# A fixed VectorE order in the last stage, earlier weight blocks spread out, and a root by Newton steps

## The chip, the cores and the metric

The kernel runs on one core of one Trainium2 chip. The metric is the time of one execution on the device in microseconds (us); the value given for a kernel is the median of its runs. In the text PE is TensorE (matrix products), DVE is VectorE, ACT is ScalarE (activation functions and copies), POOL is GpSimd, SP is the engine that issues most data transfers (DMAs). A tile here is 128 partitions of up to 512 float32 values for each of two halves of the 256 channels. "L712" is line 712 of the kernel before.

## The reference

The input is x of shape (2, 256, 64, 64) in float32. Two layers follow one another, each added to its own input, each after a group norm with 32 groups (8 channels to a group):

```python
x = x + layer0(group_norm(x))   # attention over 4096 positions, 8 heads of 32 channels
x = x + layer1(group_norm(x))   # grid attention, block attention, and a 3x3 convolution
```

Layer 0 is full attention: q, k, v by 1x1 convolutions, softmax over all 4096 positions, sums over v. Layer 1 computes q, k, v again, then

```python
ctx   = attention over positions (h % 8, w % 8) of each grid      # 64 groups of 64 tokens
feats = relu(bn(lr_W @ ctx))
qx = relu(bn(fq2 @ relu(bn(fq1 @ feats)))); kx = the same with fk1, fk2; vx = fv @ feats
out_att  = relu(bn(sr_W @ attention(qx, kx, vx)))                 # within 8x8 blocks
out_conv = conv3x3(fc(q, k, v heads), dep_w)
result   = rate1 * out_att + rate2 * out_conv
```

A group norm is `(x - mean) / sqrt(var + 1e-5)`, with mean and variance over 8 channels and all positions. Its root is computed per channel on 128 partitions, for the first 128 channels and for the second 128 channels apart.

## The kernel before, in words

The two batches are worked through one after the other, b = 0 and b = 1, and each has three stages.

Stage 1, attention of layer 0 (lines 400 to 920). PE makes the scores into a ring of PSUM banks (L594), ACT takes their exponentials (L600), PE sums them over v (L609), and DVE adds up the exponentials for the row sums (L646). Sixteen groups (8 heads, two halves of the queries) of 32 steps; `last` is the last group, and `at_block(last, j, f)` puts the work f behind step j of it. The order on PE, ACT and DVE is the order of the program (`manual_schedule`); on other engines a scheduler decides. While the last groups run, DVE gathers the statistics of the first 128 channels of layer 1's group norm: their mean and variance (`mean_of_first`, `variance_of_first`) are there by step 12. When the last scores have been taken, `before_last_rows` computes the root of the variance, its reciprocal and the shift `-mean * rstd`, and starts the normalisation of these channels (`Groups.normalise`, three tiles on POOL, five on ACT by `by_act`), while PE makes the last row sums. `behind_last_rows` takes the reciprocal of the row sums on DVE, copies them on ACT, and gives ACT the rest of the normalisations. The second 128 channels need the last head, so their mean, variance and root (`Stats.deviations`, L368) come after it. In batch 0 PE then multiplies weight matrices into each other (`fold_products`, L270 to L299: transposes, a copy on ACT called turned_w, products called pm_w) and DVE prepares the convolution's weights (prep, L984).

ACT holds one table of functions. Sqrt and Exp are in different ones, so a switch puts a table load on ACT, which the profile shows as ACT_TABLE_LOAD. The small tile `warm` is used to cause such a load ahead of time (L397 with Exp).

Stage 2, grid attention (`layer1_first`), follows for the 8 tiles: projections py (L1389), scores, softmax, feats.

Stage 3, `layer1_second`, runs over 8 tiles t of 512 positions (8 blocks of 64). Each makes hidden rows phq and phk, rows prq and prk, the values vs, scores sp, the softmax (nm, e, den, e on DVE with the exponential on ACT), its transpose at, the block matrix bd (DVE), and the result pc into res. Between these pieces PE runs convolution steps: `conv()` calls at up to three spots of a tile. The convolution is of Winograd form. Batch 0 uses F(2,3) along the rows and columns: 16 steps (strip s, column q). Batch 1 uses a wider form along the columns: 12 steps, c0 to c11, in the order (0,0)...(0,5),(1,5)...(1,0). One `conv()` issues the transform of the next step and the products of this one:

- col: POOL makes a difference of image columns, DVE finishes it with three operations (batch 1, L1155 to L1160), and there is one col buffer
- v: POOL makes four row terms of col (L1165)
- mm: 32 products on PE (L1180 for batch 1, L1062 for batch 0), into one PSUM tile of four banks, which must have been read before the next step writes it
- z: a copy on ACT and four operations on DVE (L1201 to L1204, batch 0 L1070 to L1073)
- additions of z into the layer's rows x, called xphase in batch 1 (L1211)

`conv_edges` then adds border terms to tile t on ACT, and `to_image` normalises a tile into the image xp. The block `with tc.manual_schedule(engines=...)` in this loop says on which engines the program order holds: PE always, DVE too where `near` holds (the last two tiles of batch 0). Elsewhere the scheduler interleaves DVE's instructions.

Batch 1's wider form needs two more sets of weights, which batch 0's stage 3 makes and stores: `wider_weights(wf, r, stage)` for r = 0 to 3, four DVE operations (L1102 to L1105) into the two halves of one staging tile and two transfers to memory (L1107, wf_more). A call must wait until the transfers of the call before have read the staging tile. Calls r = 0 and 1 come behind tile 3, r = 2 and 3 behind tile 4.

Of the kernel before, what the change touches and what calls it, by code (L numbers as in the profile page):

```python
# [35 lines left out]


ROWSUM_LO, ROWSUM_HI = 1e-18, 1e18


@with_exitstack
def direct_layers(ctx: ExitStack, tc: tile.TileContext, a: dict, out: bass.AP, bad: bass.AP):
# [102 lines left out]
    eps = const.tile([P, 1], F32, name="eps")  # L145
    nc.gpsimd.memset(eps, 1e-5)
    warm = const.tile([P, 1], F32, name="warm")

    def load_const(name, shape, src, behind=None):
        t = const.tile(shape, F32, name=name)  # L150
# [370 lines left out]
    def attention0(b, xts, held):  # L521
# [187 lines left out]

        def before_last_rows():  # L710

            nc.scalar.activation(st.rstd[:, first_chunk], st.d[:, first_chunk], AF.Sqrt, bias=eps)  # L712
            for t in range(2):
                st.tile(1, t)
            nc.vector.reciprocal(st.rstd[:, first_chunk], st.rstd[:, first_chunk])
            st.shift = small.tile([P, KC], F32, tag="gn_shift", name=f"shift_{b}")
            shift_of(st, 0)
            held["groups"] = Groups(es, xts, st)
            for t in range(NT - N_POOL, NT):
                held["groups"].normalise(0, t, nc.gpsimd)  # L720
            held["by_act"] = iter(range(NT - N_POOL))
            by_act(2)

        def by_act(n):
            for t in itertools.islice(held["by_act"], n):
                held["groups"].normalise(0, t, nc.scalar)

        def behind_last_rows(g):

            avs = copied[g] = w4([P, 2, T], f"avs_{b}_{g}")  # L730
            kept = held["kept"] = w4([P, T], f"kept_{b}")
            held["y"] = avs[:, 0, :]
            for part, at in enumerate(held["rows"]):
                n = slice(part * T // 2, (part + 1) * T // 2)
                for made in (nc.vector.reciprocal(avs[:, 1, n], ring[:, at, n]), nc.scalar.copy(kept[:, n], ring[:, at, n])):
                    for other in rows_made[1 - part]:
                        tc.declare_no_dep(made.ins, other.ins, reason="another bank of the ring")
                by_act(1 + part)
            for t in range(2, NT // 2):
                st.tile(1, t)  # L740

# [73 lines left out]
        at_block(last, 6, lambda: wanted.append(mean_of_first))  # L815
        at_block(last, 11, lambda: st.spread(first_chunk))
        at_block(last, 12, lambda: wanted.append(variance_of_first))

        for t in range(NT):
            if t >= NT // 2:  # L820
# [667 lines left out]
    def layer1_second(b, xts, feats, mean, rstd, shift, pacc, following):  # L1488
# [83 lines left out]
        for t in range(NT):  # L1572
            nt = f"sr_{b}_{t}"
            f = [
                feats[k][:, 8 * t : 8 * t + 8].rearrange("p o d e -> p (o d e)") for k in range(KC)
            ]

            def hidden(one, col1, nm):
                hid = w4([P, KC, T], f"h{nm}_{nt}")
                ph = [bank([P, T], f"ph{nm}_{nt}_{m}") for m in range(KC)]  # L1580
                for k, m in ((0, 0), (0, 1), (1, 0), (1, 1)) if t == 0 else ((0, 0), (1, 0), (0, 1), (1, 1)):
                    nc.tensor.matmul(  # L1582
                        ph[m], wts[one][:, k, m * P : (m + 1) * P], f[k], start=k == 0, stop=k == KC - 1
                    )
                    if k == KC - 1:
                        kept["rows"] = bn_relu(hid[:, m, :], ph[m], col1, m)
                return hid

            def branch(one, two, col1, col2, nm, between=None):
                hid = hids.pop(nm, None) or hidden(one, col1, nm)  # L1590
                if between:
                    between()
                res = w4([P, KC, T], f"r{nm}_{nt}")
                pr = [bank([P, T], f"pr{nm}_{nt}_{m}") for m in range(KC)]
                for k in range(KC):
                    for m in range(KC):
                        nc.tensor.matmul(  # L1597
                            pr[m], wts[two][:, k, m * P : (m + 1) * P], hid[:, k, :], start=k == 0, stop=k == KC - 1
                        )
                for m in range(KC):  # L1600
                    bn_relu(res[:, m, :], pr[m], col2, m)
                return res

            E = mybir.EngineType
            seam = b == 0 and t == NT - 1
            near = b == 0 and t >= NT - 2

            def step(n=1):
                for _ in range(n if near else 0):
                    next(then)  # L1610

            with tc.manual_schedule(engines={E.PE, E.DVE} if near else {E.PE}):
                hids = {}
                if t == 0:
                    hids = {"q": hidden("fq1", V_FQ1, "q"), "k": hidden("fk1", V_FK1, "k")}
                q = branch("fq1", "fq2", V_FQ1, V_FQ2, "q")
                if pending:
                    next(pending)
                    next(pending, None)
                    pending = None  # L1620
                with tc.issue_after(kept["rows"].ins):
                    for tt in images.get(t, ()):
                        to_image(tt)
                if 0 in spots.get(t, ()) and (b or t > 2):
                    conv(step if seam else None)
                if seam:
                    for n in sorted(results):
                        give(n)
                k = branch("fk1", "fk2", V_FK1, V_FK2, "k", step if seam else None)
                in_x = b and t % 4 == 0  # L1630
                res = xpool.tile([P, KC, T], F32, tag="x", name=f"res_{nt}") if in_x else w4([P, KC, T], f"res_{nt}")

                def to_res(m, pc, res=res):

                    bn_relu(
                        res[:, m, :].rearrange("p (d o e) -> p o d e", d=8, o=8),
                        pc.rearrange("p (o d e) -> p o d e", o=8, d=8), V_SRW, m,
                    )

                parts = group_attention(  # L1640
                    nt, q, k, lambda c, w, f=f: f[c][:, w * P : (w + 1) * P], wts["fv"], to_res, apart=t + 1 < NT,
                    split=t + 1 == NT, fill=lambda m: step(3 if seam else 0),
                )
                if seam:
                    step(5)
                if b == 0 and t == 2:
                    conv(behind_drain=lambda: next(parts))
                else:
                    next(parts)
                step()  # L1650
                if 1 in spots.get(t, ()):
                    conv(None if t < 2 and b == 0 else lambda: next(parts))
                elif b or t > 1:
                    next(parts)
                if t < 2 and b == 0:
                    pending = parts
                else:
                    if seam:
                        step(2)
                    next(parts, None)  # L1660
                    if seam:
                        for _ in then:
                            pass
                if 2 in spots.get(t, ()):
                    conv(step)
            if b == 0 and t == 1:


                with tc.issue_after(kept["seam"]):
                    kept["bias"] = conv_weights()  # L1670
                with tc.issue_after(kept["made"].ins):
                    for k in range(KC):
                        nc.vector.memset(xp[:, k, 0, :], 0.0)
                ahead[0] = conv_transform(b, xp, *turns[0])
            for tt in ((), (0, 1))[t] if b == 0 and t < 2 else (t,):
                conv_edges(xts, tt)
            if b == B - 1 and t == 2:
                report()
            results[t] = res
            if b:  # L1680
                for m in range(KC):
                    nc.vector.tensor_scalar(res[:, m, :], res[:, m, :], wts["rate1"], None, ALU.mult)
            if b == 0 and t in (3, 4):
                if t == 3:
                    stage = xpool.tile([P, KC, T], F32, tag="x", name="stage")
                with tc.issue_after(kept["bd"].ins):
                    for r in range(2 * (t - 3), 2 * (t - 3) + 2):
                        wider_weights(wf, r, stage)
            for n in sorted(n for n in results if done >= (NQ * (n // 4 + 1) if b else 4 * (n // 2 + 1))):
                give(n)  # L1690
            if b == 0 and t == NT - 3:
                next(then)
# [625 lines left out]
```

## Time and profile before

| | |
|---|---|
| median of 3 runs | 3011.64 us (3008.14 to 3016.84) |
| profiled execution | 3011.38 us, span 3009.5 us |
| PE | busy 2945.0 us (98%), 25043 matmuls |
| DVE | busy 2499.7 us (83%) |
| ACT | busy 2336.1 us (78%) |
| POOL | busy 815.0 us (27%) |
| PE's mean granted clock | 0.995 |
| DMA | 431.82 MB, mean 143 GB/s |

How to read it: the span is the time from the first to the last instruction that the profile sees, and the execution's own time has 1.9 us around it. A timeline line gives start and length in us, the engine, the line, the operation, the tiles written and read, how many instructions it stands for, and in brackets the idle time of the engine before it with what ended it. PEld is the load of weights into PE, which overlaps its products. The granted clock is the share of PE's full clock that it was allowed.

Stage 1 of batch 0 runs from about 113 to 1126 us, that of batch 1 to about 2637 us. Batch 0's convolution products lie between about 1300 and 1540 us, batch 1's between 2758 us and the end.

### The profile page before, as it was taken

To read this page: it belongs to the slowest core of one execution; us is meant where nothing else is said; L and a number is where in the kernel's file an instruction comes from. 1 tells how busy PE (TensorE), PEld (TensorE's weight loads), DVE (VectorE), ACT (ScalarE), POOL (GpSimd) and SP (SyncE) were. 2 spreads that over 40 slices of the span, in tenths; PEclk is the share of its full clock that TensorE was granted. 3 is DMA by queue.
4 is the path that set the end of the run, shared out by engine and by line. 5 is a ranking of instruction groups with operands and counts; after the bars stand their busy time and mean duration, and the time that the engine had idled before them with its cause. 6 is when DMAs were issued, how large, how long until landed. Compare 5 with 4: busy or idle time off the path is not lost.

```text
span 3009.5 us, 63901 instructions
## 1 busy us (share of the span) xinstructions
PE 2945.0 (98%) x25043; PEld 1830.7 (61%) x25043; DVE 2499.7 (83%) x3196; ACT 2336.1 (78%) x3283; POOL 815.0 (27%) x910
## 2 busy tenths in 40 slices
PE   7999999999999999998999999999999999998998
PEld 4555556665565656676765565566655656566665
DVE  4698998999899999956655989989998989955874
ACT  2699999999999994532235999999999999943433
POOL 1022222322222221065400232223222222213430
PEclk9999999999999999999999999999999999999999
DMA  7979778897888761231249797788978877720010
GB/s 257 277 139 184 148 157 168 160 190 149 164 181 161 154 145 43 62 139 64 63 171 264 147 182 146 163 166 162 187 147 170 176 156 151 154 69 22 15 57 30
DMA packets 254660, 431.82 MB, mean 143 GB/s; under 512 B 99416, under 2 KB 118668, under 8 KB 252172
## 3 DMA queue, kind: packets, MB, share of 16 engines
q0 software_dynamic: 96960, 237.57, 41.2%
q1 hardware_dynamic: 157244, 189.81, 23.1%
q8 instruction: 198, 3.24, 0.4%
q14 instruction: 114, 0.93, 0.1%
q10 hardware_dynamic: 144, 0.26, 0.0%
HBM read 124.27 MB, written 70.48 MB: 65 GB/s over the span
## 4 chain that ended last, share of the span: by engine, by line
PE 86%; DVE 6%; DMA 4%; ACT 2%; POOL 1%; issue 1%; SPq 0%; ACTq 0%; POOLq 0%; DVEq 0%
PE ring L594 32%; PE av L609 30%; PE mm L1062 3%; PE mm L1180 3%; PE p_wk L457 2%; PE p_wq L457 2%; DVE prep L984 2%; PE pv L483 2%; PE prq_sr L1597 1%; PE prk_sr L1597 1%; PE phk_sr L1582 1%; PE phq_sr L1582 1%; PE pvs_sr L1252 1%; DMA acc<-v 1%; PE ring L609 1%; PE pvs_lr L1252 1%
## 5 line engine op out<-in xcount | busy, mean ns | idle before, releaser
L600 ACT ACTIVATE es<-ring 128x512 f32<-128x512 f32 (+2 forms) x1574 | 1201.5, 906 | 35.8 <-PE ring L594 21.3
L594 PE MATMUL ring<-q,k 128*128 128x512 f32 x4096 | 1082.8, 407 | 7.9 <-ACT es L600 5.1
L646 DVE TENSOR_TENSOR e<-e,es 128x1024 f32<-128x1024 f32 (+1 forms) x942 | 1029.0, 1153 | 28.5 <-ACT es L600 27.0
L594 PEld LDWEIGHTS ring<-q,k 128*128 128x128 f32 x4096 | 731.3, 188 | 382.6 <-ACT es L600 116.8
L600 ACT ACTIVATE v<-ring 128x512 f32<-128x512 f32 (+2 forms) x1036 | 785.1, 892 | 17.2 <-PE ring L594 7.7
L609 PE MATMUL av<-es,v 128*32 128x256 f32 (+1 forms) x9648 | 722.5, 389 | 0.0
L646 DVE TENSOR_TENSOR e<-e,v 128x1024 f32<-128x1024 f32 (+1 forms) x624 | 669.1, 1128 | 15.5 <-ACT v L600 15.0
L609 PE MATMUL av<-v 128*32 128x256 f32 x6224 | 506.1, 389 | 0.0
L609 PEld LDWEIGHTS av<-es,v 128*32 128x32 f32 x9648 | 325.1, 109 | 263.3 <-issue 104.5
L609 PEld LDWEIGHTS av<-v 128*32 128x32 f32 x6224 | 222.2, 109 | 169.9 <-issue 70.4
L656 POOL DMA_DIRECT2D es<-es x116 | 99.0, 854 | 442.1 <-ACT es L600 419.1
L656 POOL DMA_DIRECT2D acc<-es x126 | 126.8, 1011 | 130.6 <-ACT es L600 42.9
L654 POOL DMA_DIRECT2D es<-es x20 | 11.4, 570 | 495.3 <-ACT es L600 390.0
L656 POOL DMA_DIRECT2D es<-v x74 | 63.3, 856 | 291.0 <-ACT v L600 259.4
L1062 PE MATMUL mm<-v,wf 128*128 128x256 f32 x512 | 118.2, 391 | 10.6 <-DVE z L1073 10.6
L656 POOL DMA_DIRECT2D v<-es x114 | 116.2, 1019 | 25.6 <-ACT es L600 12.2
L1062 PEld LDWEIGHTS mm<-v,wf 128*128 128x128 f32 x512 | 99.5, 196 | 28.7 <-issue 14.5
L656 POOL DMA_DIRECT2D acc<-v x86 | 88.2, 1026 | 83.6 <-DMA acc<-es 37.8
L1052 POOL TENSOR_TENSOR v<-col 128x512 f32<-128x512 f32 x64 | 83.6, 1334 | 88.3 <-DVE x L1086 33.9
L1180 PE MATMUL mm<-v,wf 128*128 128x256 f32 x384 | 85.6, 381 | 2.6 <-issue 2.6
L984 DVE SCALAR_TENSOR_TENSOR prep<-prep 128x256 f32<-128x256 f32 x198 | 83.6, 477 | 0.4
L1165 POOL TENSOR_TENSOR v<-col 128x512 f32<-128x512 f32 x48 | 59.9, 1282 | 86.1 <-DVE col L1160 86.1
(281 smaller groups left out, 2790.2 us busy)
## 6 DMA issues: line engine op xcount, KB each, us to landing
acc<-es POOLq DMA_DIRECT2D x122, 512.0 KB, 6.2
acc<-v POOLq DMA_DIRECT2D x78, 512.0 KB, 6.4
es<-es POOLq DMA_DIRECT2D x136, 256.0 KB, 4.0
v<-es POOLq DMA_DIRECT2D x134, 256.0 KB, 5.2
k<-wk_halves SPq DMA_DIRECT2D x64, 512.0 KB
q<-wq_halves SPq DMA_DIRECT2D x256, 128.0 KB
v<-v POOLq DMA_DIRECT2D x88, 256.0 KB, 5.0
es<-v POOLq DMA_DIRECT2D x86, 256.0 KB, 4.2
```

The costliest lines, as they stand in the source:

```text
L457: made = nc.tensor.matmul(pq, w0[nm][:, k, g * P : (g + 1) * P], xn[:, k, n], start=k == 0, stop=k == KC - 1)
L483: nc.tensor.matmul(pv[:, j, :], xn[:, k, n0 : n0 + P], w0["wv0"][:, k, :], start=k == 0, stop=k == KC - 1)
L594: touch(nc.tensor.matmul(sc[:, i, :], held["k", g // 2][:, j * P : (j + 1) * P], held["q", g, u // 2][:, u % 2, :], start=True, stop=True, ...
L600: nc.scalar.activation(dst, sc, AF.Exp, scale=SC0), set(range(at % BANKS, at % BANKS + m))
L609: note(nc.tensor.matmul(dst[HD0 * u : HD0 * u + HD0, n], lhs, rhs(u)[:, n], start=start, stop=stop))
L646: nc.vector.tensor_add(dst[:, s, :], dst[:, s, :], src)
L656: nc.gpsimd.dma_start(out=dst, in_=src, accum_op=ALU.add)
L984: nc.vector.scalar_tensor_tensor(acc, src, s, acc, ALU.mult, ALU.add)
L1052: (nc.gpsimd.tensor_add if plus else nc.gpsimd.tensor_sub)(dst, rows(one), rows(two))
L1062: nc.tensor.matmul(mm[:, m, r, :], wf[:, k, 4 * r + q, m * P : (m + 1) * P], v[r // 2][:, r % 2, k, :], start=k == 0, stop=k == KC - 1,)
L1180: nc.tensor.matmul(mm[:, r, :, m, :], wide.of(q)[:, k, r, m * P : (m + 1) * P], v[r // 2][:, r % 2, k, :], start=k == 0, stop=k == KC - 1,)
L1252: nc.tensor.matmul(pv[:, i, :], tokens(c, 2 * half + i), wv[:, c, :], start=c == 0, stop=c == KC - 1)
```

## The change

The diff has four parts.

- Table at the start: an activation of `warm` with Sqrt is ACT's first work.
- Root of the first 128 channels: no longer by ACT in `before_last_rows`, but by `root_of_first`, twelve small DVE operations behind step 18 of the last group: the variance plus eps, times -0.5, a first value from the bits of the number, four Newton steps of two operations, and the shift. An activation of `warm` with Sqrt now stands in `behind_last_rows`, behind all of ACT's normalisations.
- `wider_weights`: one call behind each of the tiles 3, 4 and 5 (r = 0, 1, 2) and r = 3 within tile 5, ahead of its second convolution spot, behind kept rows. The scheduler places them on DVE.
- `manual_schedule` for PE and DVE in all tiles of batch 1, so that DVE follows the order of the program there.

```diff
@@ start
     warm = const.tile([P, 1], F32, name="warm")
+    nc.scalar.activation(warm, eps, AF.Sqrt)
@@ before_last_rows
-            nc.scalar.activation(st.rstd[:, first_chunk], st.d[:, first_chunk], AF.Sqrt, bias=eps)
             for t in range(2):
                 st.tile(1, t)
-            nc.vector.reciprocal(st.rstd[:, first_chunk], st.rstd[:, first_chunk])
-            st.shift = small.tile([P, KC], F32, tag="gn_shift", name=f"shift_{b}")
-            shift_of(st, 0)
@@ new
+        def root_of_first():
+
+            part = small.tile([P, 6], F32, tag="gn_some", name=f"root_{b}")
+            y, half, u = st.rstd[:, first_chunk], part[:, 0:1], part[:, 1:2]
+            nc.vector.tensor_scalar(u, st.d[:, first_chunk], EPS, None, ALU.add)
+            nc.vector.tensor_scalar(half, u, -0.5, None, ALU.mult)
+            nc.vector.tensor_scalar(y.bitcast(I32), u.bitcast(I32), -0.5, ROOT_SEED, ALU.mult, ALU.add)
+            for _ in range(4):
+                nc.vector.scalar_tensor_tensor(u, y, y, half, ALU.mult, ALU.mult)
+                nc.vector.scalar_tensor_tensor(y, u, 1.5, y, ALU.add, ALU.mult)
+            st.shift = small.tile([P, KC], F32, tag="gn_shift", name=f"shift_{b}")
+            shift_of(st, 0)
@@ behind_last_rows
                 by_act(1 + part)
+            nc.scalar.activation(warm, eps, AF.Sqrt)
@@ plan of the last group
+        at_block(last, 18, root_of_first)
@@ layer1_second, loop over tiles
-            with tc.manual_schedule(engines={E.PE, E.DVE} if near else {E.PE}):
+            with tc.manual_schedule(engines={E.PE, E.DVE} if near or b else {E.PE}):
...
                     conv(step if seam else None)
+                if b == 0 and t == 5:
+                    with tc.issue_after(kept["rows"].ins):
+                        wider_weights(wf, 3, stage)
...
-            if b == 0 and t in (3, 4):
+            if b == 0 and 3 <= t < 6:
                 if t == 3:
                     stage = xpool.tile([P, KC, T], F32, tag="x", name="stage")
                 with tc.issue_after(kept["bd"].ins):
-                    for r in range(2 * (t - 3), 2 * (t - 3) + 2):
-                        wider_weights(wf, r, stage)
+                    wider_weights(wf, t - 3, stage)
```

More of the change, by code (lines that the diff above doesn't have):

```diff
@@ L38 @@
 ROWSUM_LO, ROWSUM_HI = 1e-18, 1e18
+EPS = 1e-5
+ROOT_SEED = float(0x5F3759DF)
 @with_exitstack
```

## The prediction, made before the result was known

> **What bounds the kernel now.** I read the page's busy shares and chain first, then looked for stretches in which TensorE (PE) is idle, since only those can be shortened.
>
> ```profile
> PE 2945.0 (98%) x25043; PEld 1830.7 (61%) x25043; DVE 2499.7 (83%) x3196; ACT 2336.1 (78%) x3283; POOL 815.0 (27%) x910
> ...
> PE 86%; DVE 6%; DMA 4%; ACT 2%; POOL 1%; issue 1%; SPq 0%; ACTq 0%; POOLq 0%; DVEq 0%
> ```
>
> PE is busy 2945.0 of 3009.5 us: no edit of other engines can win more than the 64.5 us left, plus what PE loses while its clock is halved. Four places are touched. The start, by the timeline:
>
> ```profile
> 21.28 1.28 ACT L368 ACT_TABLE_LOAD   x1 [1.29 <-PE pv_l L365]
> 22.58 0.26 ACT L368 ACTIVATE rstd_l<-pv_l,eps 128x2 f32<-128x2 f32 x1
> 23.76 6.63 PE L457 MATMUL p_wk<-xn,wqk 128*128 128x512 f32 x11 [2.57 <-DVE xn L406]
> ```
>
> The first root waits for a table load that begins only when its input is there; PE idles 2.57 us. The end of batch 0's attention, same view:
>
> ```profile
> 1124.93 1.28 ACT L712 ACT_TABLE_LOAD   x1
> ...
> 1132.55 2.39 ACT L1361 ACTIVATE es<-x,shift,rstd_l 128x512 f32<-128x512 f32 x2
> 1134.72 0.69 ACT L277 COPY turned_w<-pt_w 128x256 f32<-128x256 f32 x2
> 1135.20 1.59 PEld L283 LDWEIGHTS pm_w<-wt_lr,turned_w 128*128 128x128 f32 x8 [0.62 <-ACT turned_w L277]
> 1140.51 5.83 PE L1389 MATMUL py<-es,wt_g 128*128 128x512 f32 x13
> ```
>
> ACT copies turned_w straight after its last normalisation, and PE waits for that copy. Batch 0's convolution, PE and then DVE:
>
> ```profile
> 1381.03 8.83 PE L1062 MATMUL mm<-v,wf 128*128 128x256 f32 x32 [2.60 <-DVE z L1073]
> ...
> 1431.19 9.94 PE L1062 MATMUL mm<-v,wf 128*128 128x256 f32 x32 [7.04 <-DVE z L1073]
> ```
>
> ```profile
> 1375.24 0.69 DVE L1102 SCALAR_TENSOR_TENSOR stage<-wf 128x512 f32<-128x512 f32 x1 [1.57 <-DMA wf_more<-stage]
> ...
> 1377.96 0.68 DVE L1070 TENSOR_TENSOR z<-z,mm 128x512 f32<-128x512 f32 x1
> ...
> 1424.52 1.61 DVE L1103 TENSOR_TENSOR stage<-wf 128x512 f32<-128x512 f32 x1 [1.11 <-DMA wf_more<-stage]
> ```
>
> Two gaps, both because z stands behind the second of two weight blocks. Batch 1's convolution, PE and DVE:
>
> ```profile
> 2769.59 0.69 PE L1308 MATMUL at_sr<-ident,e_sr 128*128 128x128 f32 x2 [3.74 <-DVE e_sr L1303]
> ...
> 2779.56 7.14 PE L1180 MATMUL mm<-v,wf 128*128 128x256 f32 x32 [2.60 <-issue]
> ```
>
> ```profile
> 2769.12 0.42 DVE L1303 TENSOR_TENSOR e_sr<-e_sr,den_sr 128x256 f32<-128x256 f32 x1
> ...
> 2778.14 0.73 DVE L1157 SCALAR_TENSOR_TENSOR col<-col,xp 128x544 f32<-128x544 f32 x1 [4.59 <-POOL col L1155]
> 2778.78 0.68 DVE L1204 TENSOR_TENSOR z<-z,mm 128x512 f32<-128x512 f32 x1
> ```
>
> Here softmax and z stand behind a col that GpSimd (POOL) has not delivered. Last, the stretches view (start:end, length, busy us of PE, PEld, DVE, ACT, POOL, then PE's granted clock):
>
> ```profile
> 23.80:27.10 3.30, 3.30 (x4) 1.44 (x5) 3.30 (x8) 0.54 (x2) 0.00 (x0) 0.50 0.25 69
> 27.20:30.00 2.80, 2.80 (x8) 1.33 (x7) 2.80 (x8) 1.99 (x4) 0.00 (x0) 1.00 0.14 46
> 1381.03:1389.80 8.77, 8.77 (x33) 7.44 (x34) 2.96 (x11) 0.90 (x4) 5.58 (x5) 0.81 0.00 0
> 2769.60:2776.90 7.30, 7.30 (x28) 5.85 (x28) 3.87 (x6) 1.36 (x2) 5.94 (x5) 0.64 0.03 12
> ```
>
> A gap of 2.57 to 3.74 us is followed by about one slow stretch: 4 matmuls in 3.30 us against 8 in 2.80 costs 1.7; the 8.83 against 6.91 for an undisturbed conv product costs 1.9; 7.30 us at clock 0.64 costs 2.6; after the 7.04 gap, 9.94 against 6.91 costs 3.0. A gap is dearer than its length.
>
> The Trainium skill ("TensorE: Matmul & The Clock Gate", section "HAM oscillation — how this bites in real kernels") puts the limit at idle gaps above about 3.4 us. This trace differs: 2.57 and 2.60 already cost the clock. By the page the gap at 1378 would be worth only itself.
>
> **The change, part by part.** The sum is made against the profiled execution, 3011.38 us (span 3009.5 and 1.9 around it), 0.26 below the median.
>
> **A, start.** The Sqrt table is loaded at about 1 us, when ACT has nothing to do until 19.28. The 1.28 in front of the first root goes, the rest of the chain (root, reciprocal, first xn, p_wk) is unchanged, so PE's gap is 1.29, and I take it that the clock stays up, as it does after the 1.04 gap at 2738: 1.28 + 1.7 = 3.0. From p_wk PE works without a break to the first scores at 112.8. Against it: loads keep the DMA engines near full from 90 to 130 us, and some SP loads of k_0 move behind vals writes. Bounds -3.0 and 0; I take **-3.0**, as the rows show PE, not a load, in front of the scores.
>
> **B, end of attention.** Root by ACT (0.30), its load (1.28), the reciprocal (0.16) go from the tail; 12 small DVE operations come at block 18. Nearest rows: L352 0.16 and L354 0.22, so 12 x 0.19 = 2.3 us on a DVE without idle time. Cover: in batch 1 its last sum ends 2636.48 and is used at 2639.62, and DVE idles 1.35 and 0.92 behind it; if that cover fails it is 2.3 per batch. ACT's normalisations start earlier, but the last two stay behind the second copy of the row sums (1132.28), which waits for DVE's reciprocal of what PE summed, so ACT still ends them at 1134.94. There the new Sqrt load and one tiny activation (1.28 + 0.20) stand before turned_w: 1134.72 becomes 1136.4, pm_w and all of PE behind it to the py move by 1.7, of which 0.2 is taken by slack between pm_w and the next mean. DVE's weight preparation behind it is on the chain too, so this passes on: **+1.5** (0 to +1.7). In batch 1 there is no turned_w; ACT idles 4.55 us before its second root, which covers the load, and PE's 1.23 wait for POOL is followed by the unchanged DVE chain to the second root: 0. Newton: 0, bounds 0 to +4.6.
>
> The skill ("ScalarE: Activation LUTs", "What ACT_TABLE_LOAD costs") counts a drain of about 1.38 us beside the 1.28. In this trace ACT's next instruction follows 1.30 us after a load starts (21.28, 22.58). With the page's drain B would be an estimated +2.9.
>
> **C, weight blocks.** Block r=0 is left alone in tile 3; r=1 and r=3 stand where r=2 and r=3 stood on DVE; r=2 comes in tile 5, its first operation after the first sum of z_2_2, the others before z_2_3. Each keeps its four DVE operations and two SP transfers. At 1375 the second block and its 1.57 wait vanish: z starts when its product is there (1374.0), ends 1376.9, before PE needs it at 1378.43. Gap 2.60 and the 1.9 of clock go: 4.5, less 0.1 for issue: **-4.4**. At 1424 DVE's order is the old one, with r=1, r=3 for r=2, r=3: the 7.04 gap stays, 0. In t=5 r=2 adds 4 x 0.69 = 2.7 before z_2_3, which now ends 1473.06 against a need at 1475.25, with 1.72 of DVE idle before it: 0, at worst +2.2. SP's two late stores stand before a batch 1 load of x that is read 20 us later. Bounds -6 (the clock's phase) to 0.
>
> **D, batch 1's convolution, DVE in program order.** Softmax now precedes the next col: e_sr_0 is done 2761.15, not 2769.54, so at_sr follows mm_0_0 at 2765.85, and without the cold clock mm_0_1 starts at 2770.45, not 2779.56: 9.1 gained. But col_0_3 now precedes z_0_1. Chain: DVE z_0_0 and four updates to 2771.7; col_0_2 (1.37 + 1.30 and a res operation) to 2775.1; POOL v_0_2 5.0 and col_0_3 2.2 to 2782.4; DVE col_0_3 2.7 to 2785.1; z_0_1 2.75 to 2787.9. PE is ready for mm_0_2 at 2783.4: a new gap of 4.6, start 2788.0 instead of 2792.72, **-4.7**, plus a cold clock of 2.8 (between the 2.6 and 3.0 above). In the same way col_0_5 stands amid z_0_3 and waits for POOL; its updates hold ACT's edge sums, which stand before hq_sr_2's second half: prq stops about 3.4, and 1.9 of clock. col_1_4 amid z_0_5 does so before hq_sr_3: 2.75 and 1.9. Old small holds (0.5, 0.6, 0.4) go. Sum: -4.7 + 2.8 + 5.3 + 4.65 - 1.5 = **+6.5**; bounds -9 (only the gain) and +11 (one more such hold, 2.75 + 1.9).
>
> **Sum:** 3011.38 - 3.0 + 1.5 - 4.4 + 6.5 = **3012.0 us**.
>
> **Rivals.** (1) D's holds don't bite, because POOL's col is there earlier than I chain it: D is -9.1 and the whole 3011.4 - 15.0 = 2996.4. For: before, POOL idled 5 to 10 us ahead of most v; against: the chain has only measured durations. (2) Slower: the col holds repeat for later tiles of D (col_1_2 amid z_1_4 too) and each cools the clock; D at +11 and the start's clock not saved (-1.3): 3011.4 - 1.3 + 1.5 - 4.4 + 11 = 3018; it exceeds 3020.6 when a further hold of this price (4.65) is added: 3023. For: the order is written the same way there; against: the PE work between is longer. (3) Newton's 2.3 lands on the exponentials in both batches: 3016.6. (4) The freed DVE time of C only moves its stall and A is eaten by the loads: 3011.4 + 1.5 + 6.5 = 3019.4.
>
> **How the numbers follow.** 0.3%, 9 us, is what a measurement can tell from no change. My sum 0.45; (1) 0.17; (2) 0.18, half of it and a little more beyond 9 us; (3) 0.10; (4) 0.10, a third beyond. Faster 0.19 (all of 1 and a little of the sum's spread), slower 0.19 (2, part of 3 and 4), same 0.62. The range reaches from the whole gain of (1), 2996, to a little short of the dearest form of (2), 3022, and leaves out the spread below the one and beyond the other, about 0.15. Around the likeliest alone it is 3005 to 3017: D's bounds with only its cold clocks gone (-6.6) or one hold more.
>
> **What would show it.** After: p_wk at about 22.5 with clock near 1; the table load between ACT's last es and turned_w in batch 0 and py about 1.5 later against its attention's end; no gap at 1378, still 7 at 1424; a gap before mm_0_2 with DVE's col just before z_0_1, and gaps within prq of tiles 2 and 3. Wrong if PE runs through mm_0_2, or if sums near the attentions' ends grow waits on DVE.

## The result and the profile after

The changed kernel takes 3019.74 us (3016.11 to 3023.61) against 3011.64: a ratio of 1.0025, interval 1.0018 to 1.0032, which is 5.4 to 9.6 us slower. That is inside the 0.3% named beforehand and inside the range, but 7.7 us above the forecast and above its own range (3005 to 3017). The profiled execution of the changed kernel took 3023.03 us, 11.65 more than that of before; the sums below explain these 11.65. It lies 3.3 us above its kernel's median, while that of before lies at its own (0.26 below), so the sums explain some 3.5 us more than the 8.1 between the medians.

The page's busy line of the changed kernel:

```profile
PE 2950.0 (98%) x25043; PEld 1831.8 (61%) x25043; DVE 2508.3 (83%) x3216; ACT 2335.0 (77%) x3283; POOL 815.7 (27%) x910
```

PE is busy 5.0 us longer in a span 11.4 us longer, with the same 25043 products. So about half of the loss is idle time. The rest is products that took longer: ahead of the last products the trace of the changed kernel has nine stretches of 3.41 us at a granted clock of 0.50 (called cold below), that of before seven, and two such stretches cost some 3.4 us.

To find where, I set the two kernels' PE products side by side (the nth product of one against the nth of the other) and took the difference of their start times at the ends of the stages:

| stage (time in the kernel before) | changed minus before, gained in the stage | forecast |
|---|---|---|
| start, to the first scores at 112 | -3.66 | A: -3.0 |
| first group of attention, 112 to 180 | +4.57 | 0 |
| rest of attention, 180 to 1125 | +0.92 | 0 |
| end of attention, 1125 to 1142 | +2.71 | B: +1.5 |
| 1142 to 1310 | +0.79 | 0 |
| gap at 1378 and its product, 1310 to 1395 | -4.50 | C: -4.4 |
| 1395 to 1450 | -0.94 | 0 |
| 1450 to 2738 | +0.06 | 0 |
| batch 1's convolution, 2738 to 2995 | +10.90 | D: +6.5 |
| behind it and around the span | +0.80 | 0 |
| sum | +11.65 | +0.6 |

Stretches of identical code differ by up to 2.5 us between profiled executions (`order_alone` below has the code of the kernel before up to 2738 and comes 2.45 us later between 1450 and 2738), so the small entries carry no meaning of their own. Four do: A's gain is given back within 70 us, B is dearer, C came as forecast, and D is dearer. B's 2.71 is hardly above that spread, but `without_order`, with the load in the same place, shows 2.70 there, and each kernel below with the load moved shows 0.32.

The start in the timeline of the changed kernel:

```profile
0.73 1.28 ACT L150 ACT_TABLE_LOAD   x1 [0.73 <-PEq L2323]
...
21.79 8.39 PE L460 MATMUL p_wk<-xn,wqk 128*128 128x512 f32 x19 [1.23 <-DVE xn L409]
```

The load is at 0.73 and PE's gap is 1.23 instead of 2.57; the 8.39 us of products are undisturbed (the first 3.3 us of them ran at clock 1.00, against 0.50 before). A did locally what was forecast. The end of batch 0's attention:

```profile
1136.74 1.28 ACT L751 ACT_TABLE_LOAD   x1
...
1138.03 0.20 ACT L751 ACTIVATE warm<-eps 128x1 f32<-128x1 f32 x1
...
1138.55 3.55 PE L286 MATMUL pm_w<-wt_lr,turned_w 128*128 128x256 f32 x8 [1.89 <-ACT turned_w L280]
```

The same products in the kernel before:

```profile
1135.20 1.99 PE L283 MATMUL pm_w<-wt_lr,turned_w 128*128 128x256 f32 x8 [0.38 <-ACT turned_w L277]
```

The Sqrt load stands in front of turned_w, PE waits 1.89 instead of 0.38, and pm_w's eight products then take 3.55 us instead of 1.99. Batch 0's convolution on PE:

```profile
1383.62 7.07 PE L1076 MATMUL mm<-v,wf 128*128 128x256 f32 x32
...
1432.02 8.35 PE L1076 MATMUL mm<-v,wf 128*128 128x256 f32 x29 [7.04 <-DVE z L1087]
```

The first of these products has no gap any more and lasts 7.07 instead of 8.83; the second still waits 7.04 for z, behind a second block that waits for the first one's transfers (1.14 us on DVE at 1425.39, 1.11 before). The line shows 29 of the second's 32 products; all 32 take 9.00 us, against 9.94 before, which is the 0.94 between 1395 and 1450: two cold stretches of 3.41 us instead of three.

Batch 1's convolution, PE and then DVE:

```profile
2770.23 7.07 PE L1194 MATMUL mm<-v,wf 128*128 128x256 f32 x32
...
2788.49 10.01 PE L1194 MATMUL mm<-v,wf 128*128 128x256 f32 x32 [5.18 <-POOL v L1179]
```

```profile
2782.88 1.36 DVE L1171 SCALAR_TENSOR_TENSOR col<-col,xp 128x544 f32<-128x544 f32 x2 [7.14 <-POOL col L1169]
2784.27 1.29 DVE L1174 TENSOR_TENSOR col<-col,xp 128x1088 f32<-128x1088 f32 x1
2785.48 0.68 DVE L1215 TENSOR_TENSOR z<-z,mm 128x512 f32<-128x512 f32 x1
```

mm_0_1 starts at 2770.23 (forecast 2770.45). Then DVE idles 7.14 us in front of col_0_3, whose difference POOL delivers only at 2782.8, with z_0_1 queued behind it; PE waits 5.18 us and mm_0_2 runs 10.01 instead of 7.07. The profile names v as PE's releaser, but v_0_2 was long there: z_0_1 ends at 2788.2, just ahead of 2788.49, and it is z that frees the PSUM tile. The later holds, in tile 2 and then in tile 5:

```profile
2820.72 0.72 DVE L1171 SCALAR_TENSOR_TENSOR col<-col,xp 128x544 f32<-128x544 f32 x1 [3.61 <-POOL col L1169]
...
2827.20 2.60 PE L1611 MATMUL prq_sr<-hq_sr,wt_fq 128*128 128x512 f32 x4 [3.04 <-ACT hq_sr L1355]
```

```profile
2926.67 5.21 POOL L1179 TENSOR_TENSOR v<-col 128x512 f32<-128x512 f32 x4 [9.68 <-DVE col L1174]
...
2930.15 9.10 DVE L1225 SCALAR_TENSOR_TENSOR xphase<-z,xphase 128x256 f32<-128x256 f32 x16
...
2931.96 2.66 POOL L1169 TENSOR_TENSOR col<-xp 128x1088 f32<-128x1088 f32 x1
2935.27 0.50 ACT L1232 ACTIVATE xphase<-xphase,edges 128x8 f32<-128x8 f32 x2 [3.33 <-DVE xphase L1225]
...
2936.49 5.40 PE L1611 MATMUL prq_sr<-hq_sr,wt_fq 128*128 128x512 f32 x8 [3.52 <-ACT hq_sr L1355]
```

In tile 2 DVE waits 3.61 us for col_0_5, and PE then 3.04 us for hq_sr. Tile 5 is a hold that the prediction didn't have. POOL's v and col run from 2926.67 to 2934.6, at the same time as DVE's 16 additions, which take 9.10 us. ACT's edge sums of 2935.27 wait for a part of these additions and begin 5.1 us after the first of them (1.6 in the kernel before), hq_sr stands behind the edge sums, and PE waits 3.52 us. The same additions in the kernel before, with POOL's v beside them for the first 0.2 us only:

```profile
2924.34 5.54 DVE L1211 SCALAR_TENSOR_TENSOR xphase<-z,xphase 128x256 f32<-128x256 f32 x16
```

The stretches view of the changed kernel (length, busy times of PE, PEld, DVE, ACT, POOL, granted clock) behind four of the gaps:

```profile
1138.50:1142.10 3.60, 3.55 (x10) 2.87 (x10) 0.95 (x4) 1.19 (x4) 3.38 (x6) 0.55 0.66 162
...
2827.00:2836.00 9.00, 8.80 (x29) 6.45 (x30) 4.22 (x10) 3.39 (x7) 4.70 (x4) 0.81 0.00 0
2865.70:2869.50 3.80, 3.75 (x13) 2.58 (x14) 3.80 (x6) 1.56 (x2) 0.00 (x0) 1.00 0.37 141
2936.40:2942.00 5.60, 5.51 (x9) 2.41 (x10) 3.64 (x11) 1.55 (x4) 0.00 (x0) 0.70 0.00 0
```

Behind the gaps of 1.89, 3.04 and 3.52 us the granted clock is 0.55, 0.81 and 0.70; behind the 1.81 of tile 3 (third row) it is 1.00.

### The profile page after: what moved, and what is told of

It is laid out like the page before. It is cut to its first block, busy times and chain, and to the rows that moved or that the text cites. A ratio compares the mean times of both kernels' runs of the same rounds, so it can differ in the third digit from the quotient of the medians.

```text
span 3020.9 us, 63923 instructions
## 1 busy us (share of the span) xinstructions
PE 2950.0 (98%) x25043; PEld 1831.8 (61%) x25043; DVE 2508.3 (83%) x3216; ACT 2335.0 (77%) x3283; POOL 815.7 (27%) x910
## 5 line engine op out<-in xcount | busy, mean ns | idle before, releaser
L657 POOL DMA_DIRECT2D es<-es x20 | 11.4, 568 | 498.2 <-ACT es L603 420.1
L1076 PEld LDWEIGHTS mm<-v,wf 128*128 128x128 f32 x512 | 97.8, 193 | 25.7 <-issue 12.4
L1194 PEld LDWEIGHTS mm<-v,wf 128*128 128x128 f32 x384 | 75.2, 198 | 18.8 <-POOL v L1179 6.0
```

The source lines that it names most:

```text
L657: nc.gpsimd.dma_start(out=dst, in_=src)
L1076: nc.tensor.matmul(mm[:, m, r, :], wf[:, k, 4 * r + q, m * P : (m + 1) * P], v[r // 2][:, r % 2, k, :], start=k == 0, stop=k == KC - 1,)
L1194: nc.tensor.matmul(mm[:, r, :, m, :], wide.of(q)[:, k, r, m * P : (m + 1) * P], v[r // 2][:, r % 2, k, :], start=k == 0, stop=k == KC - 1,)
```

## The experiments

All ratios are against the kernel before, timed beside the experiment on the same chip, with 95% intervals.

**The parts apart.** The first question was whether D alone makes the loss. `order_alone` is the kernel before with D, `without_order` the changed kernel without it.

```diff
-            with tc.manual_schedule(engines={E.PE, E.DVE} if near else {E.PE}):
+            with tc.manual_schedule(engines={E.PE, E.DVE} if near or b else {E.PE}):
```

> The kernel before with one part of the change alone: program order on DVE in batch 1's last stage. Theory 1 (the order costs the time): c2 starts about 4 us earlier than before, but gaps of about 5.2, 3.0, 1.8 and 3.5 us stand in front of c2, in prq of tiles 2, 3 and 5, and the end comes 11 us later: 3022 to 3023 against 3011.6. Theory 2 (the order is harmless and the loss comes from the table loads, the Newton steps or the transfers): within 3 us of before. Theory 3 (my sum on record): +6.5.

> The changed kernel with the last stage's DVE order left to the scheduler as before. Theory 1: the rest of the change nets to about nothing (start and its give-back +1.8, end of batch 0's attention +2.2, a wait for a weight transfer +1.2, weight blocks -4.5): 3009 to 3014. Theory 2: it keeps the whole loss, 3018 to 3020.

`order_alone`: 3021.45 us, 1.0024 (1.0014 to 1.0034), and +10.0 us between 2738 and 2995 in the comparison of products. `without_order`: 3010.57 us, 0.9993 (0.9984 to 1.0003), and +0.15 there. D is the whole of the measured loss; the other three parts together are nothing that can be measured. How large D is the timing leaves open: 4.2 to 10.2 us for `order_alone`, which contains the 6.5 of the forecast as well as the 10 of its profile (taken 2.2 us above its median). The products of `order_alone` show the same gap as the changed kernel:

```profile
2790.41 9.07 PE L1180 MATMUL mm<-v,wf 128*128 128x256 f32 x32 [5.17 <-POOL v L1165]
```

**The col in front of z.** The order written in the program puts z_0_1 ahead of the transform that makes col_0_3, but a `manual_schedule` block holds the order only inside its tile, and the next tile's first col had been placed ahead of z of the tile before. `order_sums_before_col` is the changed kernel with the table load of B moved (under "B's table load" below) and with each transform of batch 1 made to follow the additions of the step before:

```diff
+                    kept["sums"] = nc.vector.scalar_tensor_tensor(xs[:, :, c, :], zs, by, ...)
...
-                ahead[done + 1] = transform(b, xp, *turns[done + 1])
+                with tc.issue_after(kept["sums"].ins) if b and done else ExitStack():
+                    ahead[done + 1] = transform(b, xp, *turns[done + 1])
```

> The kernel of the run with the early load and without the order, now again with program order on DVE in batch 1's last stage, but each col's DVE work (and its POOL work) is put behind the additions of the step before, so that no z and no addition stands behind a col that POOL has not delivered. Theory 1 (the order costs its time only through z and the additions behind a late col): from c0 to the end it takes 6 to 9 us less than the 250.8 of before instead of 10 to 11 more, since the gain of 9.3 at c1 stays and c2 starts near 2783 on before's time base; the whole is 3000 to 3006. Rival (any fixed order loses against the scheduler here, through POOL's v running late or slowing DVE's additions): c0 to the end stays above 250.8, the whole 3010 to 3020.

3007.18 us, 0.9980 (0.9971 to 0.9990), a gain, but short of the 3000 to 3006 expected. Its PE products:

```profile
2770.12 7.07 PE L1194 MATMUL mm<-v,wf 128*128 128x256 f32 x32
...
2783.04 7.07 PE L1194 MATMUL mm<-v,wf 128*128 128x256 f32 x32
...
2818.80 3.67 PE L1612 MATMUL prq_sr<-hq_sr,wt_fq 128*128 128x512 f32 x4 [2.78 <-ACT hq_sr L1355]
```

mm_0_2 follows without a gap and at 7.07, so the gain at mm_0_1 stays (9.36 us at both products, against 9.35 at mm_0_1 and 4.0 at the first product of mm_0_2 in the changed kernel). DVE makes z at 2778.16 and col behind its additions:

```profile
2778.16 0.69 DVE L1215 TENSOR_TENSOR z<-z,mm 128x512 f32<-128x512 f32 x1 [2.54 <-ACT z L1212]
...
2787.98 1.35 DVE L1171 SCALAR_TENSOR_TENSOR col<-col,xp 128x544 f32<-128x544 f32 x2
```

So the col did hold z, and the 5.18 gap with its cold clock was that. But of the 9.36 only 2.2 remain at 2941: 5.0 are lost in tile 2 (the 2.78 wait for hq_sr above) and 2.4 in tile 5 (2.09), where only the order against the edge sums was left as it was.

**The edge sums in front of hq_sr.** ACT's border terms of a tile (`conv_edges`) wait for the last additions. `combined` joins the kernel above, the weight blocks over four tiles and the late fetch (both below); `combined_edges_later` leaves out the late fetch and makes the border terms of tiles 1 and 4 follow the next tile's q branch:

```diff
+                while edges_due:
+                    with tc.issue_after(kept["rows"].ins):
+                        conv_edges(xts, edges_due.pop())
...
+            if b and t in (1, 4):
+                edges_due.append(t)
+                edged = ()
```

> All three of these together. Theory 1: the gains add, since they lie in stages that follow one another: -3 (start), -9 (blocks), -7 (order), 0 to +1 (end of attention): 2992 to 2998. Rival: only the blocks' gain stays, 3001 to 3006.

> The combined kernel without the moved fetch, and ACT's edge sums of tiles 1 and 4 in batch 1 put behind the next tile's hidden rows, so that hq of tiles 2 and 5 no longer stands behind DVE's additions. Theory 1: the gaps of 2.8 and 2.1 us in prq of these tiles go, with the half clock behind them (together 7 us by the combined run's drift from 17.7 to 10.5): 2993 to 2996 against 3001 for the combined kernel. Rival: PE then waits for DVE or POOL a little later (v of the next step) and at most half of it is won: 2997 to 3000.

`combined`: 3001.02 us, 0.9962 (0.9948 to 0.9976), short of the expected 2992 to 2998 and in the rival's range: the gains do not all add. `combined_edges_later`: 2995.02 us, 0.9942 (0.9925 to 0.9958). In `combined` the products lose 3.3 us between 2780 and 2827 and 3.9 more by 2941; in `combined_edges_later` 0.2 and 1.4. With both holds gone D is worth -7.7 us between 2738 and 2995, near the -9.1 of the first rival. What stood in the way was what DVE and ACT had queued, not the time that the engines need: in `combined_edges_later` the sixteen additions of a step still take up to 9.36 us beside POOL, and PE has one wait over 0.3 us left there, 1.38 for rk_sr.

**B's table load.** `without_order_load_early` is `without_order` with the Sqrt load at the start of the tail, where ACT's root used to be:

```diff
@@ before_last_rows
+            nc.scalar.activation(warm, eps, AF.Sqrt)
@@ behind_last_rows
-            nc.scalar.activation(warm, eps, AF.Sqrt)
```

> As the run without the order, and the Sqrt load (with its tiny activation) moved from behind ACT's last normalisation to the start of the tail, where the kernel before had its load. Theory 1: turned_w no longer waits, PE's 1.89 us gap in front of pm_w is 0.4 again, and this stage gives back 1.5 to 2.2 us: 3007 to 3012. Rival: the load in the early place holds the first normalisations instead, and nothing is gained.

3009.61 us, 0.9987 (0.9978 to 0.9997).

```profile
1131.28 1.28 ACT L715 ACT_TABLE_LOAD   x1
...
1141.55 1.99 PE L286 MATMUL pm_w<-wt_lr,turned_w 128*128 128x256 f32 x8 [0.37 <-ACT turned_w L280]
```

PE waits 0.37 for turned_w, pm_w takes 1.99, and the products lose 0.3 us between 1125 and 1142 instead of 2.7. That the load's place was the cause is shown in the profile; in the timed runs the 1 us between this and `without_order` is within the intervals.

**Newton's steps alone.** `newton_alone` is the kernel before with the steps, and the load where the root was.

```diff
-            nc.scalar.activation(st.rstd[:, first_chunk], st.d[:, first_chunk], AF.Sqrt, bias=eps)
+            nc.scalar.activation(warm, eps, AF.Sqrt)
...
+        at_block(last, 18, root_of_first)
```

> The kernel before with the Newton steps alone; the Sqrt load stays at its old place at the start of the tail. Theory 1 (my step: the twelve small operations are covered): within 2 us of before at the end of each attention, total 3010 to 3014. Rival: 2.3 us later in each batch, 3016.

3015.66 us, 1.0011 (1.0002 to 1.0021). Its twelve operations take 0.14 to 0.22 us each, 2.3 in all, as forecast, and no wait follows them: products lose 0.3 us between 1125 and 1142, and 1.24 in all by 2738. The median lies outside the 3010 to 3014 that was expected and near the rival's 3016, but the timed loss of 0.6 to 6.3 us isn't found in this one profile, and whether the steps cost something stays open.

**The weight blocks.** `blocks_over_four_tiles` is `without_order_load_early` with one block behind each of the tiles 2 to 5:

```diff
-                if b == 0 and t == 5:
-                    with tc.issue_after(kept["rows"].ins):
-                        wider_weights(wf, 3, stage)
...
-            if b == 0 and 3 <= t < 6:
-                if t == 3:
+            if b == 0 and 2 <= t < 6:
+                if t == 2:
...
-                    wider_weights(wf, t - 3, stage)
+                    wider_weights(wf, t - 2, stage)
```

> The kernel of the run with the early load and without the order, with one weight block behind each of the tiles 2, 3, 4 and 5 (none within tile 5). Theory 1 (the 7.04 us gap in tile 4 comes from the second block in front of z): this gap and the half clock behind it go, 8 to 10 us less in batch 0's last stage, the whole 3000 to 3004. Rival (the gap comes from DVE's operations slowed beside POOL in that tile, and the freed block only fills up): the gap shrinks by the block's own 4 us at most or comes again in another tile, 3005 to 3010.

3002.22 us, 0.9964 (0.9952 to 0.9977).

```profile
1411.50 7.07 PE L1076 MATMUL mm<-v,wf 128*128 128x256 f32 x32
...
1426.03 7.14 PE L1076 MATMUL mm<-v,wf 128*128 128x256 f32 x32 [2.31 <-DVE z L1087]
```

Where the changed kernel waited 7.04 us and then ran 8.35 us, this one waits 2.31 and runs 7.14. Its products gain 12.0 us between 1310 and 1450, those of `without_order` 5.4. The second block in front of z is the cost: in the changed kernel it takes 4.97 us on DVE from its first operation (1423.57) to z (1428.54), of which 1.14 is its wait for the first one's transfers. With one block in a tile it is gone, and 2.31 us of waiting for z are left. In part the 12.0 is luck: in `combined`, `combined_edges_later` and `all_four` the same wait (2.32 to 2.33) is followed by a cold stretch and the product takes 8.83, 1.7 more than here.

**The start alone.** `start_alone` is the kernel before with A's one line.

> The kernel before with the early Sqrt load at the start alone. Theory 1 (transfers bound the first attention group): p_wk starts 3 us earlier, the first scores come 3.7 us earlier, but the end of the first group, at 178.5 us before, is not earlier by more than 1 us and may be 1 us later; total 3009 to 3014. Rival (my step on record): the 3.0 us stay, total 3008.6, and the lateness of the first group in the changed kernel is chance or belongs to the moved k_0 loads, which this kernel may not have.

3012.49 us, 0.9993 (0.9984 to 1.0003): its first scores are 4.11 us earlier, and at 180 only 0.47 are left in the profile (the timed interval, -4.8 to +0.9 us, could not tell 0 from -3). Where they go is seen on ACT, and on POOL's queue of the in-memory row sums (an exponential tile is added to acc by a DMA, and may be overwritten only then):

```profile
136.85 6.52 ACT L601 ACTIVATE es<-ring 128x1536 f32<-128x1536 f32 x7 [1.06 <-DMA acc<-es]
...
146.32 3.28 ACT L601 ACTIVATE v<-ring 128x1536 f32<-128x1536 f32 x3 [1.06 <-DMA acc<-v]
...
160.80 3.84 ACT L601 ACTIVATE v<-ring 128x1536 f32<-128x1536 f32 x5 [1.33 <-DMA acc<-v]
```

```profile
134.91 0.90 POOL L657 DMA_DIRECT2D es<-v  x1 [9.31 <-DMA v<-es]
```

The second sum on POOL's queue is ordered only when the first has landed, 9.31 us later, and ACT waits 1.06, 1.06 and 1.33 us for this and what follows, 3.45 in all, near the 3.64 that the products lose there. In the kernel before ACT has no wait for a DMA between 112 and 180. The stretches view of `start_alone` (the last two columns are the DMA engines' busy share and GB/s):

```profile
110.00:120.00 10.00, 9.13 (x63) 4.83 (x65) 7.37 (x7) 10.00 (x14) 0.00 (x0) 1.00 1.05 331
...
130.00:140.00 10.00, 9.99 (x95) 5.92 (x94) 9.51 (x10) 8.94 (x13) 2.65 (x3) 1.00 1.19 225
...
170.00:180.00 10.00, 10.00 (x108) 5.88 (x106) 10.00 (x10) 8.84 (x12) 0.00 (x0) 1.00 0.08 16
```

The DMA engines are full before the first sum is ordered at 123.18 (1.05 between 110 and 120) and stay near it to 170 (0.96 between 160 and 170); then the share is 0.08. My reading was that the sums queue behind the projections' transfers, so that the first group ends when the DMA engines have caught up, however early it began.

Two runs tried that reading. `start_late_fetch` takes the next head's k off the queue in this time, `start_fewer_memory_sums` takes one of the six in-memory steps of the first group to DVE:

```diff
-                if j == 4 and g % 2 == 0 and g // 2 + 1 < NH0:
+                if j == (4 if g else 20) and g % 2 == 0 and g // 2 + 1 < NH0:
                     fetch_head(b, g // 2 + 1, held)
```

```diff
-        return SUMMED if g else SUMMED[1:]
+        return SUMMED if g else SUMMED[2:]
```

> The kernel with the early Sqrt load at the start alone, and the second head's k and v fetched behind step 20 instead of step 4 of the first group, so that 2.5 MB leave the first half of that group. Theory 1 (transfers bound the first group): the group takes 65 to 67 us from its first exponential instead of 68.8, and the start's 3 us are kept: 3008 to 3010 against 3011.6. Rival (ACT, DVE and PE bound it, and its length in these kernels is chance): the group stays at 68 to 70.

> The kernel with the early Sqrt load at the start alone, and in the first group of each batch the row sums of step 7 made by DVE instead of added in memory (five steps in memory instead of six). In the run with the moved fetch the fetch did not move on SP, so that run told nothing. Theory 1 (in-memory sums, queued behind the projections' 8 MB, land at a time of their own and hold the ring places that the exponentials write): the wait of ACT for an acc landing near 140 us goes and the first group takes 65 to 67 us from its first exponential, the whole 3007 to 3010. Rival (DVE becomes the bound, four more additions of some 1.15 us on an engine that is full until 140): the group stays at 68 to 70 us.

`start_late_fetch`: 3011.86 us, 1.0002 (0.9992 to 1.0011). It says nothing on the question: SP's fetch of k started at 120.88 (119.17 in `start_alone`) although it stands sixteen steps later in the program, because SP waits only 0.6 us in all for other transfers there. The edit didn't move what it was to move. `start_fewer_memory_sums`: 3006.50 us, 0.9982 (0.9973 to 0.9992), and ACT in the same stretch has no wait:

```profile
134.64 8.36 ACT L601 ACTIVATE es<-ring 128x512 f32<-128x512 f32 x10
142.86 5.21 ACT L601 ACTIVATE v<-ring 128x1024 f32<-128x1024 f32 x6
```

Its products are 3.55 us early at 112 and 3.56 at 180. So the gain of A was lost in the waits for in-memory sums; that these stand behind the projections' transfers is argued from the DMA share and not shown. `all_four` below repeats it: it differs from `combined_edges_later` in this edit alone, and at 180 its products are 3.41 us early against 0.06 late. What the edit does without the early load was not run. Each against the kernel before timed beside it, the medians of this run and of `start_alone` lie 6.3 and 1.4 us lower. The 4.9 between them is more than the 3.6 kept here: 2.8 come between 1640 and 1660, in batch 1's first group, which has one such sum less too and where the kernel before has a wait of ACT for one (3.11 us) and a gap of PE (1.76). In this run ACT's longest such wait there is 0.61, and PE has no such gap.

**All four.** `all_four` is `combined_edges_later` with the fewer in-memory sums: one load early at the start, Newton's steps with the Sqrt load at the tail's start, one weight block in each of four tiles, and DVE's order with z ahead of the next col and late border terms.

> The combined kernel with the later edge sums, and step 7's row sums of the first group of each batch made by DVE instead of in memory. Theory 1 (each repair acts in a stage of its own): the start's 3.5 to 4 us, given back in the kernel without this, stay: 2990 to 2992 against 2995.0, some 20 us under the kernel before. Rival: the later stages take the gain back, 2994 to 2996.

2988.20 us, 0.9919 (0.9905 to 0.9934): 24 us faster than the kernel before timed beside it, a little below the 2990 to 2992 expected, and by the two ratios some 32 us below the changed kernel. The busy line of its page:

```profile
PE 2934.7 (98%) x25043; PEld 1825.6 (61%) x25043; DVE 2521.4 (84%) x3220; ACT 2333.4 (78%) x3283; POOL 812.2 (27%) x904
```

PE is busy 15.3 us less than in the changed kernel, with the same number of products. Most of that is clock regained: ahead of the last products one cold stretch of 3.41 us is left of nine, which is worth 13.7 us.

## Why the prediction was right or wrong

- **A, -3.0 forecast, about 0 found.** The gap (1.23), the clock (1.00) and the earlier first scores came as worked out. The step that failed is "the rows show PE, not a load, in front of the scores": true at 112.8, but I looked no further. The waits of ACT for in-memory sums came next, 2.19, 0.54 and 1.62 us between 136 and 162, and took all of it. The bound of 0 and the fourth rival ("A is eaten by the loads") had it; the loads in question are not SP's, which I named, but POOL's in-memory sums.
- **B, +1.5 forecast, +2.7 found.** The load's delay of turned_w is 1.5 in the gap (1.89 against 0.38). The term left out is the clock behind this gap, 1.6 us: pm_w took 3.55 instead of 1.99. I had that price from gaps of 2.57 and more, and didn't try it on the gap that I had just worked out. The +2.9 estimated with a drain is near the 2.7 by chance: turned_w followed 1.40 us after the load's start, and the rest is the cold products. Newton's steps were hidden as far as a profile shows.
- **C, -4.4 forecast, -4.5 found.** Both halves held: the gap at 1378 with its cold clock went, and the 7.04 gap stayed. The first half of the fourth rival (the stall only moves) fell.
- **D, +6.5 forecast, +10.9 found.** The chain for the first hold was right: z_0_1 ended at 2788.2 (forecast 2787.9), with the cold product 2.9 dearer (2.8). Measured from 2738: -4.0 at mm_0_2's first product (forecast -4.7), +2.9 to mm_0_3 (+2.8), +4.5 in tile 2 (+5.3), +1.9 in tile 3 (+4.65, as this gap was 1.81 and not 2.75, and the clock stayed full). The step that failed is the count of holds: +5.6 came in tile 5, which I had put only into the bound ("one more such hold"). I had taken DVE's additions at their old length; beside POOL's v and col they took 9.10 instead of 5.54. The trace of before had this price already: sixteen additions took 6.81 us with 1.5 us of POOL's work beside them and 8.14 with 3.1. "Old small holds go", -1.5, is not to be seen apart. The +10.9 is one profile, that of `order_alone` shows +10.0; the timing can't tell either from 6.5.
- **The price of a gap.** "A gap of 2.57 to 3.74 us is followed by about one slow stretch" doesn't hold for all rows that the prediction shows: behind the gap of 2.60 at 2779.56 the product took 7.14, behind the equally long one at 1381.03 it took 8.83. It isn't the length alone that decides (last section).
- **The rivals.** The first (no holds, 2996.4) fell, but `combined_edges_later` shows it was the order, not POOL's speed, that stood against it (-7.7 for D). The second (further holds, each with its clock) came about in part: D at its bound of +11, in tile 5 instead of tile 1. The third (Newton's steps in the way) isn't settled by a profile that shows no wait and a timing of +0.11%. The fourth gave 3019.4, the nearest number, for half of the right reason.
- **The sum.** The median lies 7.7 above the forecast; that it is still within the range, and that the change still counts as none, owes more to the width allowed for the rivals than to the sum (the interval's upper end, 9.6, is past the 9 named beforehand). The forecast for the profiled execution was missed by 11.0: A and the first group 3.9, B 1.2, D 4.4, and 1.5 in stretches of unchanged code, the end and the surroundings of the span. The large errors lie on one side: each is a wait, or a slower clock, that came next after the one I had followed to its end. Only the size of tile 3's hold erred the other way.

## What to carry to other kernels

When a change starts a stage earlier, follow the next wait in it to the end of that stage, on the queue that delivers last: time gained in front of a queue that is behind is given back. When an order is fixed, look at both sides of every block's edge, for an operation that waits for another engine and stands in front of one that frees the bottleneck's buffer; ordering that pair, with B's load moved, took the same change from 0.25% slower to 0.20% faster, and left both holds that were not ordered. Price a new gap of PE with the clock behind it, as a chance and not as a certainty, and DVE's work by what POOL does beside it.

## What the runs showed of the hardware

- A gap of 1.89 us on PE was followed by clock 0.55 and cost 1.6 us more than itself; one of 1.81 us left the clock at 1.00. The Trainium skill ("TensorE: Matmul & The Clock Gate", section "HAM oscillation — how this bites in real kernels") names idle gaps above about 3.4 us; the measurement decides, and here shorter ones count.
- The length of a gap doesn't settle it: 2.31 us in `blocks_over_four_tiles` left the clock at 1.00, 2.32 at the same place in `combined` didn't. In all fourteen traces the granted clock changes only in steps of 3.41 us. Of the steps at full clock, all 46 in which PE was idle, by its products' times in the trace, for 2.0 us or more were followed by one at 0.50, 6 of the 27 with 1.48 to 2.0, and none of the 12076 with less. So a gap of 2 to 3 us cools the clock when it falls into one step, and may not when it is split over two.
- Sixteen additions of batch 1's convolution took 5.44 to 5.46 us on DVE with nothing of POOL's beside them (27 groups). In the fourteen traces 64 such groups had 1 us or more of POOL's v and col beside them, and each took 0.81 to 0.94 us longer for each us of that: 6.81 with 1.5 and 8.14 with 3.1 in `before`, 9.10 with 4.4 and 9.61 with 4.9 in the changed kernel.
- An ACT table load is followed by the next instruction 1.29 us after its start (1136.74, then 1138.03), straight behind an activation that ended at 1136.73, and 1.30 at the start, where ACT had done nothing before it.
- While the DMA engines' share was near 1 an in-memory sum was followed by the next only after 9.31 us, and the exponentials that overwrite its source waited.
